# Keeping the projected image on chip between two layers of a convolution-and-attention kernel

## The chip, the cores and the metric

The kernel runs on one core of one Trainium2 chip. The metric is device time in microseconds (us), the median of several runs. Engines are named as in the profile: PE (TensorE matmul), PEld (its weight load), DVE (VectorE), ACT (ScalarE), POOL (GpSimd), SP (SyncE, which here only issues transfers). DMA transfers are issued by SP, ACT or POOL.

## The reference

Layer 0 is attention over patches with a convolution in front, layer 1 a three-fold windowed product. Cut to what matters (x is 1 x 48 x 256 x 256, float32):

```
def _L0_conv_ref(x, w_qkv, w_dw, temperature, w_proj):
    qkv = einsum('bchw,oc->bohw', x, w_qkv); qkv = dwconv3x3(qkv, w_dw)
    q, k, v = heads(unfold 4x4 patches)          # 8 heads, 96 values a patch
    attn = softmax(einsum('bhcn,bhcm->bhnm', l2norm(q), l2norm(k)) * temperature)
    out = fold(einsum('bhcn,bhnm->bhcm', v, attn))
    return einsum('bchw,oc->bohw', out, w_proj)

def _L1_conv_ref(x, Ws, Hs, Cs, ws=64):
    xb = x.reshape(B, C, H // ws, ws, W // ws, ws)
    return einsum('bcphqw,twW,thH,tcC->bCpHqW', xb, Ws, Hs, Cs)   # three terms t

x = x + _L0_conv_ref(_gn(x), ...)     # _gn: mean and variance of 3 channels each
x = x + _L1_conv_ref(_gn(x), ...)
```

The first sum is called x1 below. Its group statistics are over the whole image, so layer 1 can't start before all of x1 is known.

## The kernel before, in words

The kernel has four stages.

1. Statistics of x, the 1x1 convolution and the depthwise convolution of head 0.
2. Attention, eight heads. Each head has 16 groups `g` of 256 patches. In each group PE makes two blocks of scores (`scores`, products on L334, exponentials on ACT, L562) and weighs the values of the group in four parts `k` (`weigh`, L591), which DVE adds up in `oaccs` (L602). Depthwise work of the next head (tiles of pool `cv`) is interleaved; in the last head there is none. `store(h, m)` (L604 on) transposes a finished part on PE (L608), copies it on ACT (L610) and sends it on POOL's queue to `os_` in DRAM (L612). The order of all instructions of this stage is written out by hand (`manual_schedule`). Keys of a head are eight tiles `kt`, of which 14 are held in pool `ah`. SP loads queries two groups ahead.
3. The projection, from L723. Eight tiles `t`, each of 16 image rows of the upper half (partitions 0 to 47) and 16 of the lower half (partitions 48 to 95). For each, SP loads `pot` (the attention output, L732) and `pxt` (x, L733), two transfers of 768 KB each; PE multiplies by `wp`, a 96 x 96 weight with two copies of the projection on its diagonal (L738, eight products of 512 columns); DVE adds the result to x in place (four adds, L745) and takes statistics (eight, L749); POOL's queue stores the sum to `x1s` in DRAM (L754). Three buffers are in rotation. Here a scheduler orders each engine's instructions. Then come the group statistics, in `group_stats` (L127 on) and once more for a layout of 64 + 48 partitions (L756 to L766), and the weights and bias of layer 1 (`csn`, L774; `cbias`, L780).
4. Layer 1, from L783. Eight units: four windows of 64 rows (`yw`) by two halves of 128 columns (`xh`). For each, SP loads x1 twice from DRAM: with channels on partitions (`load_x`, `lxq`, L807, two units ahead) and with image rows on partitions (`load_rows`, `lrt`, L816). `over_c` multiplies over channels (PE, L833) and DVE evicts the result less the bias (L840), in 11 chunks. `over_w` multiplies over columns (PE, L855) and ACT evicts (L862). `over_h` multiplies over rows (PE, L872); `residual` adds `lrt` on DVE (L884) and POOL's queue sends the sum out (L887). The order is written out by hand: a unit has three parts `q` of two `over_w` each, with the chunks of the next unit's `over_c` between them, and `over_h` of a part stands behind the following part (`late`).

Every DMA issue waits on its own engine for what it needs and holds back what is behind it on that engine's queue. DMA issues of SP and ACT signal through one set of eight semaphores, used in turn, and an issue waits until the transfer that used its semaphore last has landed.

Of the kernel before, what the change touches and what calls it, by code (L numbers as in the profile page):

```python
# [45 lines left out]
def conv_preact_kernel(  # L46
# [36 lines left out]
    make_identity(nc, ident)  # L83
    ones = const.tile([C, 128], F32, name="ones")
# [11 lines left out]
    wp = const.tile([P2, P2], F32, name="wp")  # L96
    nc.vector.memset(wp, 0.0)
    for s in range(2):
        r = slice(s * C, (s + 1) * C)
        for h in range(NH if s == 0 else H0):  # L100
            o = s * M0 + h * HC if h < H0 else (h - H0) * HC
            nc.gpsimd.dma_start(
                out=(wq[r] if h < H0 else wr[0:C])[:, o : o + HC].rearrange("c (z e) -> c z e", z=3),
                in_=w_qkvT.rearrange("c (z h e) -> h c z e", z=3, h=NH)[h],
            )
        nc.gpsimd.dma_start(out=wp[r, r], in_=w_projT)
# [11 lines left out]
    mean1 = const.tile([P2, 1], F32, name="mean1")  # L118
    rstd1 = const.tile([P2, 1], F32, name="rstd1")
# [7 lines left out]
    def group_stats(st, mean, rstd, pool, pspool):  # L127

        mv = pool.tile([P2, 2], F32, name="mv")
        nc.vector.bn_aggr(mv, st.rearrange("p n s -> p (n s)"))  # L130
        pm = pspool.tile([P2, 1], F32, name="pm", tag="pstat")
        nc.tensor.matmul(pm, lhsT=gm, rhs=mv[:, 0:1], start=True, stop=True)
        nc.vector.tensor_copy(mean, pm)
        d = pool.tile([P2, 1], F32, name="gsd")
        nc.vector.tensor_sub(d, mv[:, 0:1], mean)
        e = pool.tile([P2, 1], F32, name="gse")
        nc.vector.scalar_tensor_tensor(e, d, d, mv[:, 1:2], ALU.mult, ALU.add)
        pv = pspool.tile([P2, 1], F32, name="pv", tag="pstat")
        nc.tensor.matmul(pv, lhsT=gm, rhs=e, start=True, stop=True)
        f = pool.tile([P2, 1], F32, name="gsf")  # L140
        nc.vector.tensor_scalar_add(f, pv, EPS)
        g = pool.tile([P2, 1], F32, name="gsg")
        nc.scalar.activation(g, f, AF.Sqrt)
        nc.vector.reciprocal(rstd, g)
        return mv, e
# [253 lines left out]
    with tc.tile_pool(name="xn", bufs=1) as xnp, tc.tile_pool(name="cst", bufs=1) as cst, tc.tile_pool(  # L399
# [19 lines left out]
        group_stats(st0, mean0, rstd0, cst, nps)  # L419
# [57 lines left out]
    cv = attention.enter_context(tc.tile_pool(name="cv", bufs=1))  # L477
# [42 lines left out]
    with tc.tile_pool(name="ahead", bufs=2) as ah, tc.tile_pool(name="ae", bufs=3) as ae, tc.tile_pool(  # L520
        name="asm", bufs=6
    ) as asm, tc.tile_pool(name="ao", bufs=1) as ao, tc.tile_pool(name="big", bufs=3, space=PSUM) as big:
        MB = 8
# [4 lines left out]
        def load_key(h, m, eng=nc.sync):  # L528
            keys[h, m] = ah.tile([128, 2, 512], F32R, name="kt", bufs=14)
            load_keys(keys[h, m], h, m, eng)  # L530
# [73 lines left out]
        def store(h, m):  # L604
# [4 lines left out]
            oo = asm.tile([HD, 512], F32, name="oo", bufs=2)  # L609
            nc.scalar.copy(oo, pt.rearrange("p i n -> p (i n)"))  # L610
            for i in range(512 // TP):
                nc.gpsimd.dma_start(  # L612
                    out=os_[m * (512 // TP) + i, h * HD : (h + 1) * HD, :], in_=oo[:, i * TP : (i + 1) * TP]
                )
# [16 lines left out]
        with tc.manual_schedule():  # L631
            load_query(0, 1)
            block = scores(0, 0)
            for h in range(NH):
                more = h + 1 < NH
                rows = {r: Depthwise(h + 1, r) for r in range(CR + 1)} if more else {}
                for g in range(NG):
                    p, d, n = rows.get(g - 2), rows.get(g - 1), rows.get(g)

                    if h == 0 and 0 < g <= 6:  # L640
                        load_value(0, g + 1)
# [39 lines left out]
                    for k in range(NK):  # L681
# [28 lines left out]
                        if g == NG - 1 and k > 0:  # L710
                            for m in range(2 * k - 2, 2 * k):
                                store(h, m)
            for m in range(6, 8):
# [5 lines left out]
    RP = TP // PX * KS  # L719
    NP = TP  # L720
    with tc.tile_pool(name="pj", bufs=3) as pj, tc.tile_pool(name="pjs", bufs=1) as pjs, tc.tile_pool(
        name="pps", bufs=3, space=PSUM
    ) as pps, tc.tile_pool(name="pp1", bufs=1, space=PSUM) as pp1:  # L723
        st1 = pjs.tile([P2, HALF * W // 512, 6], F32, name="st1")
        ov = os_.rearrange("t (c k) n -> t c k n", k=KK)
        for t in range(HALF // RP):
            ot = pj.tile([P2, KK, NP], F32, name="pot")
            xt = pj.tile([P2, RP, W], F32, name="pxt")
            for s in range(2):
                r = slice(s * C, (s + 1) * C)  # L730
                y0 = s * HALF + t * RP
                nc.sync.dma_start(out=ot[r], in_=ov[s * (NT // 2 // TP) + t])  # L732
                nc.sync.dma_start(out=xt[r], in_=xc[:, y0 : y0 + RP, :])  # L733
            xv = xt.rearrange("p (py ki) (px kj) -> p ki kj py px", ki=KS, kj=KS)
            for ki in range(KS):
                ps = pps.tile([P2, KS, NP], F32, name="pps")
                for i in range(0, KS, 2):
                    nc.tensor.matmul(  # L738
                        ps[:, i : i + 2, :],
                        lhsT=wp,  # L740
                        rhs=ot[:, ki * KS + i : ki * KS + i + 2, :],
                        start=True,
                        stop=True,
                    )
                nc.vector.tensor_add(  # L745
                    xv[:, ki], ps.rearrange("p k (py px) -> p k py px", py=RP // KS), xv[:, ki]
                )
            for i in range(0, RP, 2):
                nc.vector.bn_stats(  # L749
                    st1[:, (t * RP + i) // 2, :], xt[:, i : i + 2, :].rearrange("p a b -> p (a b)")  # L750
                )
            for s in range(2):
                y0 = s * HALF + t * RP
                nc.gpsimd.dma_start(out=x1s[:, y0 : y0 + RP, :], in_=xt[s * C : (s + 1) * C])  # L754

        gm2 = pjs.tile([P2, 64 + C], F32, name="gm2")  # L756
        nc.vector.memset(gm2, 0.0)
        for o in (0, 64):
            nc.vector.tensor_copy(gm2[:, o : o + C], gm[:, 0:C])
        mv1, e1 = group_stats(st1, mean1, rstd1, pjs, pp1)  # L760
        pc1 = pp1.tile([64 + C, 1], F32, name="pc1", tag="pstat")
        nc.tensor.matmul(pc1, lhsT=gm2, rhs=e1, start=True, stop=True)
        rstd2 = l1c.tile([64 + C, 1], F32, name="rstd2")
        nc.vector.tensor_scalar_add(rstd2, pc1, EPS)
        nc.scalar.activation(rstd2, rstd2, AF.Sqrt)
        nc.vector.reciprocal(rstd2, rstd2)  # L766

        csn = l1c.tile([64 + C, T3 * C], F32, name="csn")
        for s in range(2):
# [4 lines left out]
            nc.vector.tensor_scalar_mul(csn[r], csn[r], rstd2[r])  # L774
# [5 lines left out]
        nc.vector.tensor_copy(cbias, pb1)  # L780


    with tc.tile_pool(name="lx", bufs=3) as lx, tc.tile_pool(name="lz", bufs=2) as lz, tc.tile_pool(  # L783
        name="lr", bufs=2
    ) as lr, tc.tile_pool(name="ly", bufs=4) as ly, tc.tile_pool(name="ps1", bufs=2, space=PSUM) as ps1, tc.tile_pool(
# [10 lines left out]
        units = [(yw, xh) for yw in range(H // WS) for xh in range(2)]  # L796
        NQ = 3
        xqs, rts, zts, blks, parts = {}, {}, {}, {}, {}

        def load_x(u):  # L800
# [3 lines left out]
            xq = lx.tile([64 + C, HW, 128], F32, name="lxq")  # L804
            for s in range(2):
                y0 = yw * WS + s * HW
                nc.sync.dma_start(out=xq[s * 64 : s * 64 + C], in_=x1s[:, y0 : y0 + HW, xcol])  # L807
            xqs[u] = xq

        def load_rows(u):  # L810

            yw, xh = units[u]
            xcol = slice(xh * 128, (xh + 1) * 128)
            rt = lr.tile([128, NQ * 8, 128], F32, name="lrt")
            for s in range(2):
                nc.sync.dma_start(  # L816
                    out=rt[s * WS : (s + 1) * WS],
                    in_=x1s[s * 24 : (s + 1) * 24, yw * WS : (yw + 1) * WS, xcol].rearrange("c y x -> y c x"),
                )
# [137 lines left out]
```

## Time and profile before

| | us |
|---|---|
| median of 3 runs (lowest, highest) | 3743.46 (3741.68, 3744.67) |
| the profiled execution, its own time | 3747.01 |
| its span, from first to last instruction | 3745.2 |
| busy in the span: PE, PEld, DVE, ACT, POOL | 3515.0, 2913.5, 2186.7, 1717.9, 548.3 |
| last product of the attention (L591) ends | 3263 |
| first product of the projection (L738) starts | 3277.4 |
| last statistics of the projection (L749) end | 3425.4 |
| first eviction of layer 1 (L840) starts | 3446.2 |
| last eviction of layer 1 (L884) starts | 3737.2 |

A row such as `3320.00:3340.00 20.00, 8.55 (x16) ...` of the busy table gives a stretch in us from the span's start, its length, the busy us of PE, PEld, DVE, ACT and POOL (with the number of instructions), then the TensorE clock that was granted as a share of full speed, the mean busy share of the 16 DMA engines (it can pass 1 where packets overlap) and the GB/s moved. A row of the chain of work gives a start, a duration and the work that the next row waited for. A matmul of float32 operands appears as two records.

### The profile page before, as it was taken

To read this page: it belongs to the slowest core of one execution; us is meant where nothing else is said; L and a number is where in the kernel's file an instruction comes from. 1 tells how busy PE (TensorE), PEld (TensorE's weight loads), DVE (VectorE), ACT (ScalarE), POOL (GpSimd) and SP (SyncE) were. 2 spreads that over 40 slices of the span, in tenths; PEclk is the share of its full clock that TensorE was granted. 3 is DMA by queue.
4 is the path that set the end of the run, shared out by engine and by line. 5 is a ranking of instruction groups with operands and counts; after the bars stand their busy time and mean duration, and the time that the engine had idled before them with its cause. 6 is when DMAs were issued, how large, how long until landed. Compare 5 with 4: busy or idle time off the path is not lost.

```text
span 3745.2 us, 100375 instructions
## 1 busy us (share of the span) xinstructions
PE 3515.0 (94%) x44252; PEld 2913.5 (78%) x44252; DVE 2186.7 (58%) x3514; ACT 1717.9 (46%) x2667; POOL 548.3 (15%) x628
## 2 busy tenths in 40 slices
PE   2869999999999999999999999999999999855998
PEld 1337777788888888888888888888888888713776
DVE  5454774189529943994499349925982222266564
ACT  0225665555545545554555455545554444300333
POOL 2040121012111211221122112201220000000011
PEclk9989999999999999999999999999999999966999
DMA  7465665433323332333233323332333100299784
GB/s 163 145 145 148 178 171 166 146 90 97 79 81 86 89 82 78 88 89 85 75 94 85 82 74 95 85 80 84 94 77 84 36 19 20 60 236 190 122 141 91
DMA packets 274147, 386.49 MB, mean 103 GB/s; under 512 B 77010, under 2 KB 211522, under 8 KB 269480
## 3 DMA queue, kind: packets, MB, share of 16 engines
q1 hardware_dynamic: 234790, 264.95, 27.2%
q0 software_dynamic: 35424, 106.40, 12.3%
q10 hardware_dynamic: 3490, 8.64, 1.1%
q8 instruction: 351, 5.75, 0.6%
q14 instruction: 92, 0.75, 0.1%
HBM read 234.76 MB, written 144.90 MB: 101 GB/s over the span
## 4 chain that ended last, share of the span: by engine, by line
PE 87%; DMA 4%; issue 1%; DVE 1%; SPq 0%; ACT 0%; POOL 0%; POOLq 0%; ACTq 0%; DVEq 0%
PE big L334 38%; PE big L591 37%; PE pb L855 4%; PE pa L833 2%; PE pc L872 2%; PE big L177 2%; DMA pxt<-in_x_dram 1%; PE pst L545 1%; PE pt L608 1%; DMA x1s<-pxt 1%; PE pn L247 1%; DMA pot<-os__70 1%; DMA kt<-qkv 0%; DVE pxt L745 0%; DMA lxq<-x1s 0%
## 5 line engine op out<-in xcount | busy, mean ns | idle before, releaser
L562 ACT ACTIVATE e<-big,nmx 128x1024 f32<-128x1024 f32 x1024 | 1144.3, 1118 | 825.7 <-PE big L334 624.2
L334 PE MATMUL big<-kt,qt 128*128 128x512 f32 x6144 | 1438.6, 393 | 28.3 <-DMA qt<-qkv 20.1
L591 PEld LDWEIGHTS big<-vn,e 128*64 128x64 f32 x32768 | 1361.8, 137 | 81.4 <-ACT e L562 45.1
L591 PE MATMUL big<-vn,e 128*64 128x96 f32 x32768 | 1419.5, 247 | 2.9 <-DVE vn L581 1.9
L334 PEld LDWEIGHTS big<-kt,qt 128*128 128x128 f32 x6144 | 1146.4, 188 | 290.0 <-issue 40.5
L602 DVE TENSOR_TENSOR oacc<-big,oacc 128x768 f32<-128x768 f32 x480 | 458.2, 955 | 703.7 <-PE big L591 703.7
L228 DVE SCALAR_TENSOR_TENSOR acc<-pad,dwt,acc 126x1024 f32<-126x1024 f32 x592 | 766.8, 1295 | 35.9 <-ACT acc L209 19.7
L286 POOL TENSOR_TENSOR ol<-o,oh 126x1024 fp32r<-126x1024 f32 x78 | 187.0, 2398 | 964.6 <-DVE ss L243 834.8
L575 DVE TENSOR_REDUCE zt<-zs 128x1 f32<-128x4 f32 x256 | 38.7, 151 | 342.3 <-ACT e L562 342.3
L562 ACT ACTIVATION_READ_ACCUMULATOR e<-big,nmx 128x1 f32 x1024 | 195.9, 191 | 0.0
L840 DVE TENSOR_TENSOR lzt<-pa,cbias 128x864 f32<-128x864 f32 (+1 forms) x88 | 137.0, 1628 | 100.0 <-PE pa L833 100.0
L862 ACT COPY lyt<-pb 128x512 f32<-128x512 f32 x144 | 84.5, 586 | 216.0 <-PE pb L855 216.0
L612 POOL DMA_DIRECT2D os__70<-oo x128 | 65.2, 515 | 598.9 <-ACT oo L610 598.8
L855 PEld LDWEIGHTS pb<-wsb,lzt 128*64 128x64 f32 x2304 | 126.2, 138 | 30.1 <-issue 21.9
L239 ACT ACTIVATE sq<-acc 126x1024 f32<-126x1024 f32 x74 | 78.3, 1058 | 152.1 <-issue 111.6
L273 DVE TENSOR_TENSOR o<-acc,y 126x1024 f32<-126x1024 f32 x74 | 147.6, 1994 | 0.0
L855 PE MATMUL pb<-wsb,lzt 128*64 128x128 f32 x2304 | 142.4, 279 | 3.3 <-issue 3.3
L738 PE MATMUL pps<-pot,wp 96*96 96x512 f32 x128 | 77.7, 775 | 69.9 <-DMA pot<-os__70 69.9
L292 POOL DMA_DIRECT2D qkv<-o x72 | 56.3, 781 | 528.0 <-DVE zu L577 483.3
L180 ACT ACTIVATE ot<-big,bias 108x1024 f32<-108x1024 f32 x64 | 71.1, 1113 | 131.0 <-PE big L177 73.2
L738 PEld LDWEIGHTS pps<-pot,wp 96*96 96x96 f32 x128 | 26.6, 216 | 120.6 <-issue 117.5
L209 ACT ACTIVATE acc<-pad,dwt 126x1024 f32<-126x1024 f32 x74 | 84.1, 1137 | 78.1 <-DMA pad<-t 78.1
(122 smaller groups left out, 1877.3 us busy)
## 6 DMA issues: line engine op xcount, KB each, us to landing
pad<-t SPq DMA_DIRECT2D x238, 254.0 KB
t<-ot SPq DMA_DIRECT2D x128, 217.7 KB
qkv<-ol POOLq DMA_DIRECT2D x78, 336.0 KB, 6.2
qkv<-oh POOLq DMA_DIRECT2D x70, 336.0 KB, 5.6
qt<-qkv SPq DMA_DIRECT2D x176, 96.0 KB
xs<-in_x_dram SPq DMA_DIRECT2D x128, 96.0 KB
os__70<-oo POOLq DMA_DIRECT2D x128, 96.0 KB, 2.1
pxt<-in_x_dram SPq DMA_DIRECT2D x16, 768.0 KB
```

The costliest lines, as they stand in the source:

```text
L209: nc.scalar.mul(self.acc, self.pad[:, 0:KS, 0:W], dwt[:, self.h, 0:1])
L228: nc.vector.scalar_tensor_tensor(self.acc, self.pad[:, dy : dy + KS, dx : dx + W], dwt[:, self.h, tap : tap + 1], self.acc, ALU.mult, ALU.add,
L273: nc.vector.tensor_tensor(self.o.rearrange("p (a b) x -> p a b x", a=KS), self.acc.rearrange("p a (x b) -> p a b x", b=KS), self.y.rearran ...
L286: eng.tensor_sub(self.ol, self.o, self.oh.bitcast(F32))
L334: nc.tensor.matmul(ps[:, i, :], lhsT=qt[:, r, q0 : q0 + 128], rhs=kts[2 * j + i][:, r // 2, :], start=(r == 0), stop=(r == 2),)
L562: nc.scalar.activation(e[:, j * 1024 : (j + 1) * 1024], ps.rearrange("p a b -> p (a b)"), AF.Exp, bias=nmx[:, b : b + 1], accum_out=zs[:, ...
L591: nc.tensor.matmul(ps[p : p + 64, j // 4, j % 4 * HD : (j % 4 + 1) * HD], lhsT=e[:, mb * 128 + p : mb * 128 + p + 64], rhs=vn, start=(i == 0),
L602: nc.vector.tensor_add(oaccs[h, k], ps[:, :, : 4 * HD], oaccs[h, k])
L738: nc.tensor.matmul(ps[:, i : i + 2, :], lhsT=wp, rhs=ot[:, ki * KS + i : ki * KS + i + 2, :], start=True, stop=True,)
L840: nc.vector.tensor_tensor(zv[:, :, y0 : y0 + n, :], pa[:, :, : n * T3 * C].rearrange("p s (y k) -> p s y k", y=n), cbias.rearrange("p (u v ...
L855: nc.tensor.matmul(pb[s * WS : (s + 1) * WS, i, :], lhsT=zts[u][:, t * C + c + i, :], rhs=wsb[:, t, :], start=True, stop=True,)
L862: nc.scalar.copy(yt[:, t, :], pb.rearrange("p i x -> p (i x)"))
```

## The change

It touches stages 2 (last head), 3 and 4.

- **x1 on chip.** In the projection a tile's two row blocks now lie on partitions 0 to 47 and 64 to 111, the layout that `over_c` reads. Tiles are taken window by window: `t = 2 w + sub`, where the two blocks are rows `w*64 + sub*16` and `w*64 + 32 + sub*16`. The sums of a window stay in `xts[w]` (32 KB a partition). Windows 0, 2 and 3 are kept until layer 1 has read them; window 1 lies in a pool that is closed after the projection and is loaded again from `x1s` at unit 1, into the place of window 0. Units take the windows in the order 0, 2, 3, 1. `load_x` is gone. All of x1 is still stored to `x1s`, for `load_rows`; the stores of windows 2 and 3 are issued behind the loop.
- **Products.** `wp` holds the projection twice, on partitions 0 and 64; each product over 96 rows becomes two over 48, into PSUM partitions 0 to 63 and 64 to 111.
- **Partitions between.** Partitions 48 to 63 of `xts` are filled with zeros, window 0 by DVE in the last head, the others by ACT.
- **Loads.** x of window 0 is loaded by SP in groups 1 to 8 of the last head, and `os_` of tiles 0 and 1 at its end, into room that convolution tiles and six of the key tiles left (pools `cv` and `kb`, now on the other side of the memory). All other loads of the projection are issued by ACT. Four `os_` tiles are in rotation; x tiles are not reused.
- **Stores of the last head.** The last three use buffers of their own.
- **Statistics.** Done once, in the layout of 112 partitions, with `gm2` loaded ahead.
- **Layer 1's order.** `over_h` of a part follows directly behind it, after one chunk of `over_c` (in the last unit, after the next `over_w`). Row loads are made for each part, three in rotation; `lyt` has three buffers in place of four.

The diff, cut to its core:

```diff
+    wp = const.tile([64 + C, 64], F32, name="wp")
 ...
-        nc.gpsimd.dma_start(out=wp[r, r], in_=w_projT)
+        nc.gpsimd.dma_start(out=wp[s * 64 : s * 64 + C, 0:C], in_=w_projT)
 ...
         def load_key(h, m, eng=nc.sync):
-            keys[h, m] = ah.tile([128, 2, 512], F32R, name="kt", bufs=14)
+            first = (h * NM + m) % 14 < 8
+            keys[h, m] = (ah if first else kb).tile([128, 2, 512], F32R, name="kt", bufs=8 if first else 6)
 ...
+                    if not more and g == 0:
+                        convolution.close()
+                        xw = ctx.enter_context(tc.tile_pool(name="xw", bufs=1, side="right"))
+                        early = ExitStack()
+                        pa = early.enter_context(tc.tile_pool(name="pa", bufs=1, side="right"))
+                        xts[0] = xw.tile([64 + C, 2 * RP, W], F32, name="xwt")
 ...
+                        if not more and 0 < g <= 2 * RP // 4 and k == 1:
+                            y = slice((g - 1) * 4, g * 4)
+                            nc.vector.memset(xts[0][32:64, y], 0.0)
+                            for s in range(2):
+                                nc.sync.dma_start(
+                                    out=xts[0][s * 64 : s * 64 + C, y],
+                                    in_=xc[:, s * 2 * RP + y.start : s * 2 * RP + y.stop, :],
+                                )
+                        if not more and g == NG - 1 and k in (1, 2):
+                            pots[k - 1] = pa.tile([64 + C, KK, TP], F32, name="pa", bufs=2)
+                            load_output(pots[k - 1], k - 1)
 ...
+            for t in range(NTP):
+                w, sub = divmod(t, 2)
+                if t > 1:
+                    pots[t] = (pj if t // 2 % 2 else pa).tile([64 + C, KK, TP], F32, name="pa", bufs=2)
+                    load_output(pots[t], t, nc.scalar)
+                if w:
+                    if sub == 0:
+                        xts[w] = (pjs if w == 1 else xk).tile([64 + C, 2 * RP, W], F32, name="xk")
+                        nc.scalar.copy(
+                            xts[w][32:64].rearrange("p a b -> p (a b)"),
+                            zero[32:64].to_broadcast([32, 2 * RP * W]),
+                        )
+                    load_input(xts[w], w, sub)
 ...
+                    for i in range(0, KS, 2):
+                        for s in range(2):
+                            m = 64 if s == 0 else C
+                            nc.tensor.matmul(
+                                ps[s * 64 : s * 64 + m, i : i + 2, :],
+                                lhsT=wp[s * 64 : s * 64 + C, 0:m],
+                                rhs=pots[t][s * 64 : s * 64 + C, ki * KS + i : ki * KS + i + 2, :],
+                                start=True,
+                                stop=True,
+                            )
 ...
+                if w < 2:
+                    store_x1(w, sub, nc.gpsimd)
+
+            for w in (2, 3):
+                for sub in range(2):
+                    store_x1(w, sub, nc.gpsimd)
+        group_stats(st1, gm2, mean1, rstd1, pjs, pp1)
 ...
-        units = [(yw, xh) for yw in range(H // WS) for xh in range(2)]
+        units = [(yw, xh) for yw in (0, 2, 3, 1) for xh in range(2)]
 ...
         with tc.manual_schedule():
-            for u in range(2):
-                load_x(u)
             for _ in over_c(0):
                 pass
-            late = None
             for u in range(len(units)):
-                load_rows(u)
-                if u + 2 < len(units):
-                    load_x(u + 2)
-                ahead = over_c(u + 1) if u + 1 < len(units) else iter(())
+                last = u + 1 == len(units)
+                if u == 1:
+                    xts[1] = xw.tile([64 + C, HW, W], F32, name="xwt")
+                    for s in range(2):
+                        nc.sync.dma_start(
+                            out=xts[1][s * 64 : s * 64 + C], in_=x1s[:, WS + s * HW : WS + (s + 1) * HW, :]
+                        )
+                ahead = iter(()) if last else over_c(u + 1)
                 for q in range(NQ):
+                    load_rows(u, q)
                     parts[u, q] = []
                     for b in range(2):
                         c0 = b * 24 + q * 8
                         parts[u, q].append(over_w(u, c0, c0 + 4))
-                        for _ in range(2):
-                            next(ahead, None)
-                    if late:
-                        over_h(*late)
-                    late = u, q
-            over_h(*late)
+                        next(ahead, None)
+                        if last and b == 0 and q:
+                            over_h(u, q - 1)
+                        if not last and b == 1:
+                            over_h(u, q)
+                        next(ahead, None)
+            over_h(len(units) - 1, NQ - 1)
```

On SP's queue the order at the end is: the four `os_` loads of tiles 0 and 1, the six row loads of unit 0, the two loads of window 1, then the other row loads. On ACT's queue: copies of the last head's parts with the two `os_` loads of tile 2 between them, then zero fill, x of tile 2, `os_` and x of tile 3, `os_` of tile 4, and so on. The buffers of the row loads lie where `os_` tiles of the projection were, and the first row load waits for the products of tile 5; the `os_` loads of tile 7 take the semaphores of the first row loads.

## Prediction, made before the run

> **What bounds the kernel now.** I read the page's slices first, then the busy table of single stretches, then the chain of work in the last fifth, then the DMA queues there.
>
> ```profile
> PE   2869999999999999999999999999999999855998
> PEclk9989999999999999999999999999999999966999
> DMA  7465665433323332333233323332333100299784
> ```
>
> Up to slice 34 PE is full at full clock. The hole is in slices 34 to 36, some 180 us, where PE is half busy at a clock of 0.6 and DMA is at 9. That is the projection, nearly all that the change touches. The busy table, taken there (busy us of PE, weight load, DVE, ACT, POOL, then PE clock, DMA share, GB/s):
>
> ```profile
> 3260.00:3270.00 10.00, 5.16 (x80) 4.66 (x79) 1.10 (x2) 2.16 (x4) 2.99 (x6) 0.88 0.60 118
> 3280.00:3300.00 20.00, 15.00 (x26) 5.24 (x25) 16.02 (x14) 0.00 (x0) 1.02 (x2) 0.71 1.00 219
> 3300.00:3320.00 20.00, 10.77 (x21) 3.56 (x19) 12.67 (x13) 0.00 (x0) 1.02 (x2) 0.74 1.04 287
> 3320.00:3340.00 20.00, 8.55 (x16) 3.10 (x16) 12.00 (x13) 0.00 (x0) 1.01 (x2) 0.66 0.99 231
> 3340.00:3360.00 20.00, 9.39 (x18) 3.19 (x17) 12.85 (x13) 0.00 (x0) 1.01 (x2) 0.66 1.01 242
> 3360.00:3380.00 20.00, 10.20 (x18) 3.52 (x17) 12.49 (x14) 0.00 (x0) 1.01 (x2) 0.66 1.00 237
> 3380.00:3400.00 20.00, 9.81 (x17) 3.37 (x16) 11.90 (x13) 0.00 (x0) 1.01 (x2) 0.66 1.01 271
> ```
>
> From 3280 to 3400 the DMA engines have no gap (share 0.99 to 1.04, mean 248 GB/s), and DVE needs 12.5 of each 20 us. So the loop is bound by bytes: 4.72 MB a tile (os_ and x in, x1 out, 1.57 MB each), a period of 20 us. The queues' shares from 3300 to 3400 price one transfer:
>
> ```profile
> q1 hardware_dynamic: 1344, 16.58, 74.5%
> q0 software_dynamic: 720, 8.77, 26.4%
> ```
>
> Loads moved 16.58 MB in 74.5 us, 222 GB/s, 7.1 us a tile; stores 8.77 MB in 26.4 us, 4.7 us a tile. After the loop the chain shows a detour:
>
> ```profile
> 3420.99 0.50 POOL x1s L754
> 3421.49 8.76 DMA x1s<-pxt
> ...
> 3430.80 13.42 DMA lxq<-x1s
> 3444.22 0.14 issue
> 3444.35 1.79 PE pa L833 x11
> 3446.15 0.02 issue
> 3446.17 1.64 DVE lzt L840
> ```
>
> x1 goes out and comes back before layer 1 may start; the statistics, ready at 3432.1 (end of cbias), are not what it waits for. From 3465 on PE is the bound again (268.6 of 275 us busy).
>
> **The change, part by part.** Times are in the profiled execution (span 3745.2 us, 3747.0 with what lies around it, 3.6 above the median of the runs, 3743.5); I subtract the sum from the median.
>
> Attention: 0. The instruction order is unchanged up to the last head, where SP gets 16 loads of 196 KB and DVE 8 memsets 32x1024 (nearest row: 0.38 us for 128x384; about 1 us each). PE is full there (150 of 150 us from 3000), DVE is busy 36 of those 150, DMA 0.08. On SP each pair waits for its memset and stands before a query load that is due more than 20 us later, one group being 21.8 us (10.71 + 11.10). Without that cover they would cost some 8 us.
>
> Projection. Its first os_ load still starts at 3260, when the first parts are stored. The last load sets the end, so I compare what DMA must move up to it. (a) The flow starts 11.0 us later than before's first x load (3248.9): +11.0. (b) Before lost 0.13 of 11 us and 0.40 of 10 us there: -5.4. (c) x of tiles 0 and 1 is already in: 2 x 7.1 = -14.1. (d) In before the last os_ tile landed at 3408.2, when tile 6's store had only been issued (3405.9); with loads four tiles ahead that store comes first: +4.7. (e) SP runs ahead: the six row loads of unit 0 (1.57 MB) wait only for tile 5's products, as their buffers lie where its operands were, so they are loaded inside the loop. The same loads in 512-byte runs moved 208 GB/s from 3455.5 to 3463.5: +7.6. Sum +3.8. The last load is now x, with the products waiting in PSUM, so the tail is four adds and eight statistics (7.6 + 4.84 = 12.4) and not 17.2 (3408.2 to 3425.4, cold products first): -4.8. Together -1.0.
>
> Bounds of this term. Above: tile 2's os_ loads on ACT wait for stores of the last head, which landed after 2.0 to 18.0 us in this stretch; ACT's own copies wait behind them, then a zero fill of 32x8192. Rows of 582 ns for 512 and 1118 ns for 1024 elements give 1.05 ns an element, 8.6 us, three times. The second and third fill have four tiles queued in front; the first may leave DMA idle 0 to 6 us. I take 0, since tile 0's store and the os_ tiles fill most of it. Also the last os_ loads must wait for the row loads' semaphores (one set of eight lanes for SP and ACT); tile 6 is still flowing then, so 0, at most 4. Below: were stores free, loads alone would take 14 x 7.1 + 7.6 = 107 us from 3262, and DVE 8 x 12.4 = 99 from its first add (about 3274): end at 3381, -44.
>
> Row: loads and stores from two issuers fill the engines to 101%, so a third issuer finds no room. The Trainium skill ("DMA: Bandwidth & Descriptors", section "Issuing engines are not separate DMA queues") says that DMAs begun by different engines run on the same 16 engines and interleave, and that this saves issue time alone; it speaks against any gain from moving the loads to ACT. By that rule the move is worth 0, as I have it; without it, up to the -44 just named.
>
> Products: 16 matmuls a tile in two 64-row, 64-column quadrants for 8 of 96x96. If each pair runs together, 8 x 2 x 0.43 = 6.8 us a tile at full clock, as now: 0, under DVE's 12.4. Adds and statistics span 112 partitions in place of 96, with as many elements in each: 0. The nearest row is the product over rows, four quadrants in turn: 24 records of 512 columns in 2.73 us, four at a time.
>
> Start of layer 1. x1 of the first window is on chip. From the end of the statistics to the first eviction: now 3446.17 - 3425.44 = 20.7. After: to cbias 6.7 (3432.1), less one product, root and reciprocal (0.8), plus the memset of wsb and gaps, about 6.8. So -13.9; bounds -10 (weights late) and -15.
>
> Layer 1's loop: the same matmuls on a full PE, 0. The product over rows right behind its part waits for ACT's last copy (0.59), but 0.8 us of other products and its first eight matmuls (1.8 us) stand before that one. At the end one eviction less is exposed (3732.99, 1.24): -1.3.
>
> A new wait: x1 rows 64 to 127 do not stay. Their reload (3.15 MB) is put on SP's queue when unit 0's last product over channels is read, at a moment X, ahead of unit 1's first row load. From the rows, unit 1's residual is wanted at X + 2.73 + 2.86 + 1.67 + 2.86 + 0.84 + 2.73 = X + 13.7. The row load lands at X + 0.9 (issue) + 14.2 + 2.5 + 2.0 (the shortest landing) = X + 19.6, if one queue serves in order. Then 1.24 for the residual and 1.63 for the eviction behind it: the PSUM buffer that PE needs at X + 18.2 comes free at X + 22.5. So +4.3 once. Bounds: 0 (the row load overtakes) and +9 (at 169 GB/s, the rate from 3445 to 3465). In-order service is seen in before: four lxq loads at 145 GB/s, then the row loads issued behind them at 208.
>
> The same page ("Queues, rings and completion order") says that on each engine a queue's descriptors are consumed in ring order; by it the wait is there, without it the term would be 0.
>
> Sum: -1.0 - 13.9 - 1.3 + 4.3 = -11.9, so 3731.6 us.
>
> **The rivals.** *DMA gives more room than its share shows.* For: deeper prefetch and no reuse of x tiles (SP waited 90 us in all for stores to free them). Against: no slice under 0.99. Wholly, -44 in place of -1.0: 3689; half of it 3710.
>
> *The start and the reload eat it* (no change). Idle of 6 at the first fill and 4 at the last lanes, the reload at +9: -11.9 + 10 + 4.7 = +2.8, 3746; half of that, 3739. For: the 18-us landing; against: all at once.
>
> *Unpaired products* (slower). If the quadrants do not overlap, 32 records a tile at 0.427 us and the clock granted from 3400 to 3450, 0.61, take 22.4 us; eight tiles from 3270.5 end at 3449.5, last add and statistics 3456, first eviction 3463: +16.9 in place of -14.9, sum +19.9, 3763; at a clock of 0.5, 27.3 us a tile and 3803. It decides from 19 us a tile, 0.59 us a record. At full clock (13.7) it costs little. Against: the 2.73-us row.
>
> *It does not do what it says*: if the row loads did not depend on tile 5, they would come earlier with the same bytes: same sum.
>
> **How the numbers follow.** Forecast (3718 to 3736) 0.50; DMA faster (below 3718) 0.15; eaten 0.23; slower, unpaired or several stalls, 0.12. A measurement here tells 0.2% from no change, 7.5 us. Faster 0.65, same 0.23, slower 0.12. The range runs from 3706, past half of the first rival, to 3744; beyond it lie some 0.06 below and 0.14 above.
>
> **What would show it.** Right: DMA share near 1 through the projection; last statistics at 3418 to 3430; first layer-1 eviction 7 us behind them; one wait of DVE for a row load of 5 to 7 us in unit 1. Wrong: gaps in DMA before tile 2 (the fill) or before the last tile (the lanes); products longer than 10 us a tile; DVE without gaps in the projection (first rival); no wait in unit 1.

## The result, and the profile after

| | before | after |
|---|---|---|
| median of the runs beside each other (lowest, highest) | 3742.79 (3737.93, 3744.67) | 3773.28 (3763.92, 3777.45) |
| ratio, 95% interval | | 1.0079 (1.0064 to 1.0094) |
| the profiled execution, its own time; span | 3747.01; 3745.2 | 3763.92; 3762.1 |
| last product of the attention ends | 3262.95 | 3276.70 |
| from there to the last statistics of the projection | 162.5 | 164.4 |
| from there to the first eviction of layer 1 | 20.7 | 7.1 |
| from there to the end of the span | 299.1 | 313.9 |

The change made the kernel slower by 0.8%, where 0.3% faster was forecast. The four stages account for the spans' difference of 16.9: +13.8 in the attention, +1.9 in the projection, -13.6 at the start of layer 1, +14.9 in layer 1. They are those of one execution on each side: the medians differ by 30.5. The profiled execution was the shortest of its five (3764 to 3777; the three longest had a mean granted clock of 0.969 to 0.970, the two shortest 0.971 and 0.972), and what the longer ones lost more is in no profile; e9 below runs the same kernel again.

The slices of the page after, the same three rows as of before:

```profile
PE   2869999999999999999999999999999999876899
PEclk9989999999999999999999999999999999976999
DMA  7465665433323332333233323332333110295543
```

The hole is narrower in DMA (one slice at 9 in place of two), but a slice of layer 1 has only 8 tenths of PE. At this scale the attention shows nothing; its loss is 0.4%. The busy table of the projection after (columns as before):

```profile
3300.00:3320.00 20.00, 15.88 (x60) 4.53 (x58) 17.94 (x15) 14.06 (x2) 1.02 (x2) 0.84 0.70 124
3320.00:3340.00 20.00, 18.04 (x58) 5.03 (x54) 19.46 (x22) 0.00 (x0) 2.01 (x4) 0.74 1.00 304
3340.00:3360.00 20.00, 11.84 (x32) 3.23 (x31) 12.46 (x12) 5.61 (x1) 1.00 (x2) 0.66 1.00 286
3360.00:3380.00 20.00, 13.60 (x38) 3.35 (x37) 14.78 (x14) 1.41 (x1) 1.00 (x2) 0.74 1.01 301
3380.00:3400.00 20.00, 10.92 (x32) 2.96 (x28) 9.93 (x12) 0.00 (x0) 1.00 (x2) 0.71 1.05 239
3400.00:3420.00 20.00, 13.26 (x32) 3.35 (x32) 12.36 (x12) 1.28 (x1) 1.00 (x2) 0.61 1.06 237
3420.00:3440.00 20.00, 3.67 (x8) 0.77 (x8) 11.38 (x11) 0.00 (x0) 1.00 (x2) 0.56 0.35 69
```

Read the last two columns: with the same share of 1.0, the engines now move 286 to 304 GB/s where the mean before was 248. So a full share was not the limit that the prediction took it for; before's own stretches, from 219 to 287 GB/s at that share, had already said so. The rate then falls to 239 and 237 (the two stretches with the row loads), and at either end there is idle time (0.70, 0.35). The queues from 3320 to 3380 say the same: 10.72 MB of loads in 67.7% of 60 us are 264 GB/s, before 222.

```profile
q10 hardware_dynamic: 876, 10.72, 67.7%
q0 software_dynamic: 575, 7.08, 32.7%
```

The chain of waits, end of the projection and start of layer 1, after:

```profile
3379.54 1.96 PE pps L806 x6
...
3383.85 27.60 DMA lrt<-x1s
...
3411.47 17.02 DMA xk<-in_x_dram
...
3428.62 7.68 DVE xk L813 x4
3436.30 4.76 DVE st L819 x8
...
3445.85 0.60 PE pb L840
3446.45 1.71 PE pa L885 x11
...
3448.19 1.64 DVE lzt L892
```

The detour over `x1s` and `lxq` is gone. In its place the last x load stands behind a row load of layer 1 (27.6 us), whose semaphore it uses next: in the trace, the row loads issued at 3383.18 and 3383.85 and the x loads of tile 7, issued at 3410.43 and 3411.47, signal the same two.

### The profile page after: what moved, and what is told of

It reads as the page before. It is cut to its first block, busy times and chain, and to the rows that moved or that the text cites. A ratio compares the mean times of both kernels' runs of the same rounds, so it can differ in the third digit from the quotient of the medians.

```text
span 3762.1 us, 100723 instructions
## 1 busy us (share of the span) xinstructions
PE 3544.7 (94%) x44378; PEld 2912.6 (77%) x44378; DVE 2195.6 (58%) x3519; ACT 1737.1 (46%) x2669; POOL 547.4 (15%) x628
## 3 DMA queue, kind: packets, MB, share of 16 engines
q1 hardware_dynamic: 209830, 236.64, 22.4%
## 4 chain that ended last, share of the span: by engine, by line
PE 80%; issue 6%; DMA 5%; DVE 1%; POOL 1%; ACT 0%; SPq 0%; ACTq 0%; POOLq 0%; DVEq 0%
PE big L336 38%; PE big L599 37%; DMA xk<-in_x_dram 2%; PE big L179 2%; DMA lrt<-x1s 1%; PE pst L553 1%; PE pt L616 1%; DMA os__70<-oo 1%; POOL out_dram L939 1%; PE pn L249 1%; PE pa L885 1%; PE pb L907 0%; DMA kt<-qkv 0%; DVE xk L813 0%; DVE lzt L892 0%
## 5 line engine op out<-in xcount | busy, mean ns | idle before, releaser
L336 PE MATMUL big<-kt,qt 128*128 128x512 f32 x6144 | 1453.9, 395 | 28.6 <-DMA kt<-qkv 28.5
L806 PE MATMUL pps<-pa,wp 48*64 48x512 f32 (+1 forms) x256 | 89.4, 813 | 50.0 <-DVE xk L813 31.2
L806 PEld LDWEIGHTS pps<-pa,wp 48*64 48x64 f32 (+1 forms) x256 | 24.0, 167 | 114.1 <-issue 50.0
```

Of the source, the lines that this page charges most:

```text
L336: nc.tensor.matmul(ps[:, i, :], lhsT=qt[:, r, q0 : q0 + 128], rhs=kts[2 * j + i][:, r // 2, :], start=(r == 0), stop=(r == 2),)
L806: nc.tensor.matmul(ps[s * 64 : s * 64 + m, i : i + 2, :], lhsT=wp[s * 64 : s * 64 + C, 0:m], rhs=pots[t][s * 64 : s * 64 + C, ki * KS + i ...
```

## The experiments

Stage times below are those of the table, read the same way, from one profiled execution of each run. Each run was timed beside the kernel before; a ratio is its median over that of the kernel before, with the 95% interval in brackets. Theory: the loss has three separate places, the keys in a second pool, the row loads inside the projection's loop, and the reload in unit 1. Rivals are named with each run.

### The keys

Trace after against trace before, from each head's first matmul of scores to the next head's: heads 1 to 6 lost 3.6, 1.6, 2.2, 2.9, 1.5 and 3.7 us, heads 0 and 7 nothing. Heads 1 to 6 hold 6, 2, 4, 4, 2 and 6 of their eight key tiles in the new pool `kb`. There, matmuls of scores start 228 to 241 ns after one another (in long runs 237 and 229 in turn), elsewhere 227. Part 5 of the page has it in one row (busy us, mean ns); before, then after:

```profile
L334 PE MATMUL big<-kt,qt 128*128 128x512 f32 x6144 | 1438.6, 393 | 28.3 <-DMA qt<-qkv 20.1
```

```profile
L336 PE MATMUL big<-kt,qt 128*128 128x512 f32 x6144 | 1453.9, 395 | 28.6 <-DMA kt<-qkv 28.5
```

The same 6144 matmuls, 15.3 us more. 24 tiles of 96 matmuls each are 2304, so 6.6 ns each.

**e1**, the kernel before with that part of the change alone:

```diff
+    kb = attention.enter_context(tc.tile_pool(name="kb", bufs=6, side="right"))
-            keys[h, m] = ah.tile([128, 2, 512], F32R, name="kt", bufs=14)
+            first = (h * NM + m) % 14 < 8
+            keys[h, m] = (ah if first else kb).tile([128, 2, 512], F32R, name="kt", bufs=8 if first else 6)
```

> The kernel before, with one part of the change alone: 6 of the 14 key buffers lie in a pool of their own at the other end of the chip's memory. Theory (the place of the keys): where the changed kernel lost 15.0 us in heads 1 to 6, each matmul of scores whose keys lie in the second pool took 237 and 229 ns in turn in place of 227 and 227; so this kernel loses about the same, 12 to 18 us, 3755 to 3761, and its attention shows the same pairs of 466 ns in the same heads, none in heads 0 and 7. Rival (the 15 us come from something else in the change, the extra loads or the order): no change, 3740 to 3746, pairs of 454 ns throughout.

Measured 3762.15 beside 3741.75, ratio 1.0061 (1.0049 to 1.0073). The last product of the attention ends 19.4 us later than before's (3.3 of it are lost ahead of the first scores), and the row of matmuls has grown by 16.2:

```profile
L334 PE MATMUL big<-kt,qt 128*128 128x512 f32 x6144 | 1454.8, 395 | 29.2 <-DMA qt<-qkv 20.1
```

The slow matmuls stand in the same heads. The place of the keys is the cause, nothing else of the change is needed.

**e2**, the changed kernel, the second pool 640 bytes lower:

```diff
+    gap = convolution.enter_context(tc.tile_pool(name="gap", bufs=1, side="right"))
+    nc.vector.memset(gap.tile([128, 160], F32, name="gap"), 0.0)
     kb = convolution.enter_context(tc.tile_pool(name="kb", bufs=6, side="right"))
```

> The changed kernel with the second pool of keys moved down by 640 bytes, so that all keys lie a multiple of 1024 bytes from the query buffers, as all 14 did before. Theory A (what matters is where keys and queries lie within 1024 bytes, against each other): the 15 us of the attention are gone, the first product of the projection comes some 15 us sooner, pairs of 454 ns; 15 us less than the changed kernel's time. Theory B (what matters is that these keys lie over 120 KB from the queries): nothing changes, pairs stay at 466 ns. Theory C (only the 64-byte or 256-byte place counts): a part of it.

Measured 1.0038 (1.0025 to 1.0051), 3754.41. The attention ends at 3264.2, and the heads that were slow have their 227 ns again:

```profile
L336 PE MATMUL big<-kt,qt 128*128 128x512 f32 x6144 | 1436.4, 393 | 29.1 <-DMA qt<-qkv 20.4
```

Theory A holds; a distance of 120 KB costs nothing, which refutes B.

**e8** and **e12**, the kernel before with a gap between queries and keys, 384 and then 256 bytes (`[128, 64]`):

```diff
         load_query(0, 0)
+        nc.vector.memset(ah.tile([128, 96], F32, name="gap", bufs=1), 0.0)
```

> The kernel before with 384 bytes left free between the query and the key buffers, nothing else. Theory (what matters is where keys and queries lie against each other within 512 or 1024 bytes): every head now shows the slower matmuls of scores, pairs of 460 to 466 ns in place of 454, 20 to 37 us more in all, 3762 to 3779. Rival (what matters is the place of the keys alone, or a distance of 120 KB): pairs of 454 ns and no change, 3740 to 3746.

> The kernel before with 256 bytes left free between the query and the key buffers, in place of the 384 that cost 33 us. So far offsets of 0 and of 512 bytes within 1024 between a key row and a query block gave 227 ns a matmul, offsets of 32, 128 and 384 bytes within 512 gave 230 to 237. Theory (only multiples of 512 are free of it): as with 384 bytes, 230 to 234 ns in all heads, 20 to 37 us more. Rival (multiples of 256 are free as well): 227 ns and no change, 3740 to 3747.

Measured with 384 bytes 3775.92, ratio 1.0088 (1.0071 to 1.0105); with 256 bytes 3743.05, ratio 1.0002 (0.9991 to 1.0013). Their rows, in that order:

```profile
L334 PE MATMUL big<-kt,qt 128*128 128x512 f32 x6144 | 1468.8, 398 | 28.7 <-DMA kt<-qkv 28.3
```

```profile
L334 PE MATMUL big<-kt,qt 128*128 128x512 f32 x6144 | 1437.5, 393 | 28.7 <-DMA qt<-qkv 20.1
```

With 384 bytes every head is slower, by 4.9 ns a matmul, some 30 us in all, from an edit that adds one small memset and moves buffers; the other large row of matmuls (L591) stays within 2 us of 1419.5. With 256 nothing happens. So e12's theory falls: a distance of 256 bytes between keys and queries is as free as a multiple of 1024. What costs, modulo 256, is 128 (640 bytes in the changed kernel, 384 in e8: 6.6 and 4.9 ns a matmul) and 32 (e1: 7.0 ns); other offsets weren't tried. These offsets come from the sizes of the tiles; no profile shows an address. By the same sizes the queries and keys of pool `ah` begin elsewhere modulo 256 in the changed kernel, where `cv` no longer lies below them, and heads 0 and 7 keep their 227 ns; that speaks for the distance between the two operands and against the place of either.

### The reload in unit 1

The waits of layer 1 after, PE's and then one of DVE's (us in total, times, longest):

```profile
PE pa L885 <- DVE lzt L892: 11.8, 6, 10.5
PE pc L924 <- issue: 2.9, 1, 2.9
...
DVE lrt L936 <- DMA lrt<-x1s: 17.3, 1, 17.3
```

And PE's timeline there:

```profile
3511.33 1.93 PE L924 MATMUL pc<-lyt,hsb 64*64 64x512 f32 x11
3516.13 1.94 PE L924 MATMUL pc<-lyt,hsb 64*64 64x512 f32 x13 [2.87 <-issue]
...
3521.79 1.01 PE L885 MATMUL pa<-csn,xk 48*128 48x144 f32 x12
3533.25 1.81 PE L885 MATMUL pa<-csn,xk 48*128 48x144 f32 x12 [10.45 <-DVE lzt L892]
```

DVE waits for the row load, so it doesn't free a PSUM buffer, and PE stands 10.45 us. The 12 matmuls behind the hole take 1.81 us in place of 1.01: the granted clock (third number from the end) was 0.57 there.

```profile
3530.00:3540.00 10.00, 6.75 (x68) 6.30 (x70) 5.86 (x4) 1.57 (x3) 1.39 (x2) 0.57 0.71 153
```

The stop inside `pc` is another thing: PE waits for nothing that the profile shows. The instruction queue (q8 of the page) moves a packet of 16 KB there (start 3513.14, 1.38 us). The packet is late: it starts 19.3 us after the one before it, where 9.1 is the median of layer 1, and it comes while data packets of 32 KB from the reload hold one DMA engine each for 2.3 to 4.1 us.

**e3**, row loads first:

```diff
                 if u == 1:
+                    for q in range(2):
+                        load_rows(u, q)
                     xts[1] = xw.tile([64 + C, HW, W], F32, name="xwt")
...
-                    load_rows(u, q)
+                    if u != 1 or q == 2:
+                        load_rows(u, q)
```

> The changed kernel with the first two row loads of unit 1 issued ahead of the reload of window 1 in place of behind it. Theory (layer 1 lost 14.9 us because the first row load of unit 1 stands behind 3.15 MB on one queue and landed 27.8 us after its issue): the one long wait of VectorE for a row load (17.3 us) goes, layer 1 from its first eviction to the end takes 299 to 302 us and not 313.9, the whole is 12 to 15 us shorter. Rival (the reload takes the DMA engines from whatever comes beside it): the third row load of unit 1, which still stands behind the reload, becomes the late one, or the first two land slowly; a gain under 5 us.

Measured 1.0055 (1.0042 to 1.0068), 3758.12. Layer 1 took 305.1, 8.8 less: between the two. No wait of DVE for a row load is left; PE's waits in layer 1 are now

```profile
PE pb L907 <- issue: 4.2, 2, 2.9
PE pc L924 <- issue: 2.6, 1, 2.6
PE pa L885 <- DVE lzt L892: 1.3, 5, 0.3
```

Two stops of 2.6 and 2.9 us, at 3510.7 and 3522.6, beside instruction packets that start at 3509.84 and 3522.29, 18.6 and 12.4 us after the one before. So the wait for the row load is shown, and a second price of the burst came out. The traces of e2, e4 and e9, which have the same reload, show the same stop once each (2.8 to 3.1 us, packet 19.0 to 19.3 us after the last). In all six cases PE goes on 1.5 to 1.7 us after the late packet has ended. The packet's own length is not the cause: one of 1.84 us in e5 and one of 1.75 in the kernel before passed without a stop. Nor is the interval alone: one of 15.3 us passed in the kernel before. That PE stopped for want of instructions is read from these coincidences, and that the 32-KB packets held them up is argued; neither is proved by itself.

### The row loads in the projection's loop

**e4** places the row buffers where tile 6's operand lay, so that their loads wait for the loop's last products:

```diff
-    with tc.tile_pool(name="lz", bufs=2) as lz, tc.tile_pool(name="lr", bufs=3) as lr,
+    with tc.tile_pool(name="lr", bufs=3) as lr, tc.tile_pool(name="lz", bufs=2) as lz,
```

> The changed kernel with the row buffers placed where the operand of tile 6 lay, so that the six row loads of unit 0 wait for the last products of the projection and no longer come inside its loop. Theory (they cost 7.6 us of the loop's DMA time, and the last x load had to wait for their semaphores until 3410): the last x load is issued some 15 to 20 us sooner, the statistics end 7 to 12 us sooner, the row loads still land before the first residual asks (3479), 7 to 12 us less. Rival (the loop's end is set by DVE and the stores anyway, or the row loads land too late for the first residual): less than 3 us, with a new wait of VectorE for a row load in unit 0.

Measured 1.0020 (1.0012 to 1.0029), 3748.92. The projection took 151.0 in place of 164.4, layer 1 314.7 (no new wait in unit 0). First adds of tiles 6 and 7 came 17.0 and 12.2 us after those of the tile before; after the change it was 22.4 and 28.7. The last x loads are issued at 3384.3 and 3388.0, and no longer at 3410.4 and 3411.5. The gain is 13.3, a little above the theory's range; how much of it is the bytes of the row loads and how much their semaphores isn't separated.

### All three together

**e5**: the edits of e2 and e4, and the reload cut into eight pieces:

```diff
                 if u == 1:
                     xts[1] = xw.tile([64 + C, HW, W], F32, name="xwt")
-                    for s in range(2):
-                        nc.sync.dma_start(
-                            out=xts[1][s * 64 : s * 64 + C], in_=x1s[:, WS + s * HW : WS + (s + 1) * HW, :]
-                        )
...
                     load_rows(u, q)
+                    piece = (u - 1) * NQ + q
+                    if 0 <= piece < 8:
+                        y = piece * HW // 8
+                        for s in range(2):
+                            nc.sync.dma_start(
+                                out=xts[1][s * 64 : s * 64 + C, y : y + HW // 8],
+                                in_=x1s[:, WS + s * HW + y : WS + s * HW + y + HW // 8, :],
+                            )
```

> The changed kernel with three remedies at once: the second pool of keys moved down by 640 bytes, the row loads of unit 0 kept out of the projection's loop, and the reload of window 1 cut into eight pieces of 4 rows a half, one behind the row loads of each part from unit 1 on. Theory (the three losses are separate stretches and add): attention ends near 3264 as before, the projection takes 147 to 152 us, from the last statistics to the first eviction 7.1, layer 1 299 to 302; span 3718 to 3725, some 20 to 25 us under the kernel before. Rival (pieces still stand in the way of stores and row loads, as the whole reload did): layer 1 303 to 307, span 3725 to 3732.

Measured 3715.57 beside 3742.89, ratio 0.9936 (0.9920 to 0.9951): faster than both kernels. Span 3711.3: attention to 3260.5, projection 146.3, start 7.1, layer 1 297.4. All PE waits of layer 1:

```profile
PE pb L909 <- issue: 1.3, 1, 1.3
PE pa L887 <- DVE lzt L894: 1.3, 5, 0.3
```

No stop of PE for a row load and none for instructions is left (DVE still waits for row loads, three times, 3.2 us in all). The three losses lie in separate stages, and the remedies don't undo one another: against the changed kernel the attention ends 16.2 us sooner (12.5 in e2), the projection is 18.1 shorter (13.3 in e4), layer 1 16.5 (8.8 in e3, with another remedy). In the loop DMA is again at 1.0, at up to 318 GB/s:

```profile
3325.00:3345.00 20.00, 16.06 (x38) 4.55 (x40) 13.89 (x15) 1.86 (x1) 1.00 (x2) 0.59 1.01 275
3345.00:3365.00 20.00, 15.43 (x50) 4.36 (x46) 13.69 (x15) 5.15 (x1) 1.00 (x2) 0.83 1.00 300
3365.00:3385.00 20.00, 14.48 (x42) 3.51 (x40) 16.34 (x15) 1.28 (x1) 1.01 (x2) 0.74 1.01 318
```

**e7**, e5 with x of tiles 0 and 1 loaded by SP at the end of the attention and not in the last head:

```diff
-                            for s in range(2):
-                                nc.sync.dma_start(
-                                    out=xts[0][s * 64 : s * 64 + C, y],
-                                    in_=xc[:, s * 2 * RP + y.start : s * 2 * RP + y.stop, :],
-                                )
...
+            for sub in range(2):
+                for s in range(2):
+                    nc.sync.dma_start(
+                        out=xts[0][s * 64 : s * 64 + C, sub * RP : (sub + 1) * RP], in_=xc[:, image_rows(0, s, sub), :]
+                    )
```

> The kernel with the three remedies, but the x of tiles 0 and 1 loaded at the end of the attention and not in the last head. Theory (the loop is bound by bytes, so the prediction's 7.1 us a tile holds): the projection gets 12 to 15 us longer. Rival (the first tiles' loads fit into the time in which the DMA engines idle ahead of tile 2's loads): 3 to 8 us.

Measured 0.9971 (0.9960 to 0.9982), 3730.22. The projection took 160.9, 14.6 more than in e5: the theory, 7.3 us a tile.

### Who issues, and how fast the loop can go

**e6**, e5 with one tile's operand loads issued by SP:

```diff
-                    load_output(pots[t], t, nc.scalar)
+                    load_output(pots[t], t, nc.sync if t == 2 else nc.scalar)
```

> The kernel with the three remedies, and the loads of tile 2's operand issued by SyncE in place of ScalarE. Theory (ScalarE stood 17.4 us in front of its last copies of the attention, since a load that waits for a store stood ahead of them; so stores, first fill and the x loads of tile 2 came late, and DMA idled some 5 us): the copies follow the transposes at once, the x loads of tile 2 are issued 3 to 5 us sooner, and the projection gets 3 to 6 us shorter. Rival (the loop is bound by bytes and the wait was hidden): less than 1.5 us.

Measured 0.9942 (0.9925 to 0.9959), 3715.88 beside e5's 3715.57. Its projection is 6.2 us shorter in the trace (140.1), its attention ends 4.3 us later; in the times nothing shows. The mechanism fell: ScalarE's copies still waited 16.0 us, not for the load but for the stores of earlier parts, whose buffer they need.

**e10**, e5 with all the loop's loads, of x and of the operand, issued by SP:

```diff
-                nc.scalar.dma_start(
+                nc.sync.dma_start(
...
-                    load_output(pots[t], t, nc.scalar)
+                    load_output(pots[t], t, nc.sync)
```

> The kernel with the three remedies, and all loads of the projection issued by SyncE, none by ScalarE. Theory (the issuing engine gives no bandwidth; the loop's rate is that of the DMA engines): the tiles of the loop follow each other as fast as with ScalarE's loads, 15 to 16.5 us apart, and since ScalarE no longer waits ahead of its copies and fills the projection takes 138 to 146 us as with tile 2's loads moved alone. Rival (a queue of its own for the loads is what made the loop faster than before): tiles 18 to 20 us apart and a projection 15 to 25 us longer.

Measured 0.9940 (0.9921 to 0.9959). Tiles 2 to 6 came 17 to 21 us apart and the projection took 151.2, which is neither theory's number; the times can't tell it from e5 or e6. The DMA engines moved 281 GB/s from 3315 to 3380, and 286 from 3305 to 3385 in e5. The Trainium skill ("DMA: Bandwidth & Descriptors", section "Issuing engines are not separate DMA queues") gives a second issuing engine no bandwidth; these rates agree with it, and the ratios of e5 and e10, 0.9936 and 0.9940, agree within their intervals. Why e10's projection is 4.9 us longer in the one trace of each stays open.

**e11**, the kernel before with five buffers for the projection's tiles:

```diff
-    with tc.tile_pool(name="pj", bufs=3) as pj, tc.tile_pool(name="pjs", bufs=1) as pjs, tc.tile_pool(
+    with tc.tile_pool(name="pj", bufs=5) as pj, tc.tile_pool(name="pjs", bufs=1) as pjs, tc.tile_pool(
```

> The kernel before with five buffers in place of three for the projection's tiles, nothing else, so that loads run four tiles ahead of the products. Theory (the 20 us a tile of the kernel before were no limit of the DMA engines but came from too few loads in flight, since each waited for a store to free its buffer): tiles follow at 15.5 to 17.5 us, the projection gets 10 to 20 us shorter. Rival (the loads' rate comes from the rows of the chip's memory that they write, 0 to 47 and 48 to 95 before, 0 to 47 and 64 to 111 after): tiles stay 19 to 20 us apart, less than 5 us gained.

Measured 1.0019 (1.0006 to 1.0031). From tile 1 to tile 6 first adds came 18.0 us apart on average (before 20.3), so depth is part of the rate, though less than the theory had it; but the first add was 6.6 us later, the projection only 1.1 us shorter, and the whole no faster. Its loads moved 17.88 MB in 74.4 us:

```profile
q1 hardware_dynamic: 1453, 17.88, 74.4%
q0 software_dynamic: 734, 9.14, 26.1%
```

That is 240 GB/s, between 222 before and 264 after. What gives the rest (other rows of the memory, another order of the tiles) stays open.

**e9**, the changed kernel again, unaltered:

> The changed kernel itself once more, unaltered, to see how its times spread beside the kernel before on one chip: five runs so far gave two at 3764 us and three at 3773 to 3777, and the profile is of a run at 3764. Theory (plain spread from run to run): times between 3760 and 3778 with no gap, and the same stages as in the first profile (attention to 3277, projection 164, layer 1 314) within 5 us. Rival (a stage that comes in two lengths): times at two levels, and a profile in which one stage is 10 us longer than it was.

Measured 3766.35 (3761.65 to 3770.01), 1.0069 (1.0053 to 1.0084); stages as in the first profile (164.4, 7.2, 315.0). The six times lie close, so nothing speaks for two levels; but none of them reaches the 3773 to 3777 of three of the first five, and what those lost stays open.

## Why the prediction was wrong

The forecast was -11.9 us, and the profiled span grew by 16.9. Of the 28.8 between them the attention has 13.8, layer 1 11.9 (14.9 where the terms give +3.0), the projection 2.9 and the start of layer 1 0.3.

**Attention: 0.** This step failed, and by the most: +13.8. "The instruction order is unchanged" was true; the duration of an instruction was taken to be unchanged with it. The change put six of 14 key buffers elsewhere, and the trace of before can't price that: all its keys lie at one offset from the queries. Here the Trainium skill would have misled too. "SBUF — State Buffer", section "Who interferes with whom", calls TensorE's two read ports, for moving data and for weights, independent; e8 and e12 differ by 128 bytes of empty memory and 33 us, so what one operand costs these matmuls does depend on where the other lies. That the two reads get in each other's way is the reading at hand; no run shows it directly.

**Start of layer 1: -13.9.** Right: 20.7 became 7.1, -13.6.

**The new wait: +4.3, bounds 0 and +9.** The mechanism was right, one wait of DVE for a row load behind the reload, at the place foretold; the size was not. Layer 1 lost 14.9, and e5 puts the whole price at 313.9 - 297.4 = 16.5. The mis-sized term is the 14.2 us for 3.15 MB, priced at the rate of the projection's loads: the reload's packets took 24.3 us, 130 GB/s, below the 169 of the upper bound, and the second of the row load's two transfers, for which DVE waited, landed 30.0 us after the moment X and not 19.6. So PE stood 10.45 us (7.5 to 8.8 in e2, e4 and e9, which have the same reload). Two prices were missing: PE's stop for instructions (2.9) and the lower clock behind the wait (0.8 us in the 12 matmuls shown, 1.6 in the 48 of `over_w` behind them).

**Projection: -1.0.** Near (+1.9) by luck: errors that cancel. Right: x of two tiles, 14.1 (e7: 14.6); the tail, 12.4 (measured 12.4 from add to last statistics). Too small: the row loads, 7.6 and 0, at most 4, for the semaphores (e4: 13.3; it was the last x loads that waited); the first fill's idle time, 0 (0.70 of 20 us is 6, the upper bound). The first add came 24.9 us after the attention's end (18.4 before), where the working of the lower bound had it after about 11. Missed: the loop's rate. First adds of tiles 2 to 5 came 16.8 us apart (3327.1 to 3377.5), in the kernel before 19.9, at the same full share. That is the first rival, "DMA gives more room", and the reason given against it, that no slice was under 0.99, did not hold.

**Products: 0.** Right. 118 of the 128 pairs start within 0.034 us of each other; unpaired products, the rival on the slower side, did not happen. The largest part of the loss, the attention's, was on no list.

**End of layer 1: -1.3.** The wait of 1.3 is gone from the list of waits, but e5's layer 1 (297.4) is no shorter than that of e1 (297.5), which has the old order. So the gain isn't seen in the stage.

## What to carry to other kernels

When buffers move, look at the addresses of both operands of the matmuls that fill the time: here it was worth 15 to 30 us to have keys and queries a multiple of 256 bytes apart. A busy share of 1.0 was no bound here (219 to 318 GB/s at that share): compare GB/s between stretches before taking it as one. A transfer that is due much later should go in small pieces behind what is due soon, and the place of a buffer decides when its load starts.

## What the runs showed of the hardware that was not expected

- Matmuls of 512 float32r columns with new weights each time start 227 ns apart, and 228 to 242 (5 to 7 more on average) if moving data and weights lie 32 or 128 bytes off a multiple of 256 from each other (e1, e8, the changed kernel).
- Packets of 32 KB into 48 partitions held a DMA engine for 2.3 to 4.1 us; the whole reload moved about 130 GB/s. Pieces in 4 KB packets (e5) went by without a stop of PE.
- PE stood 2.6 to 3.1 us in the middle of a run of matmuls while such packets were in flight, six times in five traces, each time until 1.5 to 1.7 us after a late instruction packet.
